# A four-layer conditional residual kernel: expert gates by way of DRAM, the place of the second group's routing, and the width of layer 3's second products

## The chip, the cores and the metric

The kernel runs on one core of a Trainium2 chip. The metric is device time in microseconds of one execution. Before the change the median of three runs is 597.46 us (597.17 to 600.03). The profiled execution took 598.18 us, of which the profile shows a span of 596.40 us on the core.

The core's engines work side by side and meet at semaphores: TensorE (PE; its weight loads are listed as PEld), VectorE (DVE), ScalarE (ACT), GpSimd (POOL), and SyncE (SP), which here only issues DMAs. Each engine does its own instructions in the order in which they were written.

## The reference

`x` has 8 sequences of 256 tokens and 1024 features. Four layers are added to it in turn. Cut to what matters:

```python
# L0: a shared matrix, plus 8 experts of rank 16, the best two of them by token
logits = einsum('btd,ed->bte', x, Wr) + 5.0 * one_hot(lang)[:, None, :]
topw, topi = top_k(logits, 2)
gates  = sum(one_hot(topi, 8) * softmax(topw)[..., None], axis=-2)
h      = einsum('btd,erd->bter', x, A)
x = x + einsum('btd,od->bto', x, W) + 2.0 * einsum('bter,bte,eor->bto', h, gates, B)
# L1: a weight plus a sign mask with a coefficient by sequence
x = x + einsum('bsi,oi->bso', x, W1) + b1 + einsum('bsi,bio->bso', x, 2 * mask - 1) * coeff
# L2: a full weight by sequence, chosen among 8 adapters
x = x + einsum('bsi,boi->bso', x, w2[ids])
# L3: rank 16 by sequence: down to 16 ranks, and up again
Bx = einsum('bni,bri->bnr', x, B3[ids])
x = x + einsum('bnr,bor->bno', Bx, A3[ids])
```

## The kernel before

**Tiling.** Features lie on partitions: `x` is 8 blocks (`K`) of 128 features. Two sequences make a pair of 512 tokens (`N`), two pairs make a group, and there are two groups. All large products are in float32r, each operand split in a high and a low part (`whi` and `wlo`, `hl`), and three of the four partial products are added up. ScalarE casts the high part (`highs`, L291), VectorE subtracts to get the low one (`lows`, L297), 4 and 3 items ahead of TensorE. The residual is folded into the weights: GpSimd adds the identity to a diagonal block (L241).

**Stages.** For each group: 16 slots of layer 0 (a product scheme with seven quarter products, `product` at L627), then for each pair 16 units of layer 1 and 16 of layer 2 (`main` at L907). A unit is one output block of 128 features for one sequence. The order is written out by hand: `l0_works` (L701) names what the other engines do at each slot, `l0_mids` (L790) what TensorE does in the middle of a slot's product, and `main` and `side` (L972) say the same by unit number `u` from 0 to 15. A work under a negative number comes ahead of that slot's casts. Pair numbers: `pair_of(g, 0)` is 1 and 3, `pair_of(g, 1)` is 0 and 2; in `l0_works` they are `p0` and `p1`.

**Gates of layer 0.** `logits` (L307) multiplies x with the router's weights in 32-column pieces of TensorE, into a PSUM bank. `router` (L318) on VectorE transposes them and finds the best two, `weigh` (L352) makes the weights, with one exponential on ScalarE, and transposes the gates to rows. The gates must then stand on 128 partitions, one for each (expert, rank). For pair 1 TensorE does that (`gates_by_transpose`). For the pairs 0, 2 and 3, `expand` (L384) writes the 128x128 tile to DRAM, and `gates_by_rank` (L401) reads it back, one DMA for each expert, the row repeated for 16 ranks. All of these DMAs are in SyncE's queue, along with weight loads, mask loads and stores. `gate` (L416) multiplies them with the experts' hidden values, `split_gates` (L409) makes the high and low part, and the `lora` products in slots 5, 9, 13 and 15 use them. In group 1 the logits of both pairs come in the last layer-2 units of the group before (q=1, u=13), router and weights at u=14 and 15, `expand` at slot 0, the reads at slots 3 and 6.

**Layer 3.** `proj_pair` (L445) and `proj` (L496) are the projections down to rank 16, also in 32-column pieces, four partial sums on four groups of partitions. `rank_pair` (L461) adds those four with a selection matrix, once for each of three blocks of 32 partitions; then the second product (`finish`, L476) multiplies 96 rows, which hold the partial products of high and low parts, 256 tokens at a time. For the pairs 0, 1 and 2 this work is put into the runs of later units or slots as `fillers`; the last pair goes by sequence and ends the kernel. `load_l3` and `prep_l3` (L428, L435) load and split the adapters, one tile for each sequence. Outputs are stored by SyncE.

PSUM has four auxiliary banks (`bank`, numbers 0 to 3) that logits, gates, experts and layer 3 share.

Of the kernel before, what the change touches and what calls it, by code (L numbers as in the profile page):

```python
# [12 lines left out]
ALU = mybir.AluOpType  # L13
# [21 lines left out]
def kernel(ctx: ExitStack, tc: tile.TileContext, x, lang, coeff, ids,  # L35
# [55 lines left out]


    sel = cst.tile([P, R], F32, name="sel")
    nc.vector.tensor_copy(sel, ident[:, :R])
    for g in range(1, 4):
        tt(sel, sel, ident[:, 32 * g:32 * g + R], ALU.add)
    sel3_raw = cst.tile([P, 96], F32, name="sel3_raw")
    nc.vector.memset(sel3_raw, 0.0)
    for c in range(3):
        nc.vector.tensor_copy(sel3_raw[:, 32 * c:32 * c + R], sel)  # L100
    sel3 = cst.tile([P, 96], FR, name="sel3")
    nc.vector.tensor_copy(sel3, sel3_raw)

# [203 lines left out]
    def logits(p):  # L307

        a, j = p // 2, 1 - p % 2
        pls[p] = bank(j, f"pl{p}")  # L310
        for k in range(K):
            for g in range(4):
                mm(pls[p][32 * g:32 * g + 32, :P], wrs[:, k, :],  # L313
                   X[a][:, j, k, g * P:(g + 1) * P], start=(k == 0), stop=(k == K - 1))
# [64 lines left out]

    gts, gates, phs, by_rank = {}, {}, {}, {}  # L380

    gts, gates, phs, by_expert = {}, {}, {}, {}

    def expand(p):  # L384

        by_expert[p] = dram.tile([P, P], F32, tag=f"gates{p}", name=f"gates{p}")
        nc.sync.dma_start(by_expert[p], gxs.pop(p))

# [12 lines left out]
    def gates_by_rank(p):  # L401

        gts[p] = gp.tile([P, N], F32, tag="lg", name=f"gt{p}", bufs=3)
        src = by_expert.pop(p).rearrange("(g e) t -> e g t", g=4)
        for e in range(E):
            nc.sync.dma_start(gts[p][e * R:(e + 1) * R].rearrange("r (g t) -> r g t", g=4),  # L406
                              src[e:e + 1].to_broadcast([R, 4, P]))

# [19 lines left out]
    def load_l3(b):  # L428
        raw = rawp.tile([96, K * P], F32, tag="w1", name=f"a3raw{b}", bufs=2)
        nc.sync.dma_start(raw, a3[bass.ds(adapter(b), 1)].rearrange("a r o -> (a r) o"))  # L430
        bt = l3p.tile([P, K, 32], F32, tag="b3", name=f"b3_{b}")
        nc.sync.dma_start(bt, b3[bass.ds(adapter(b), 1)].rearrange("a p k r -> (a p) k r"))
        l3raw[b], l3b[b] = raw, bt

    def prep_l3(b):  # L435
        raw = l3raw.pop(b)
        at = l3p.tile([96, K * P], FR, tag="a3", name=f"a3_{b}")
        copy(at, raw)
        tt(at[64:96, :], raw[64:96, :], f32(at[64:96, :]), ALU.subtract)
        l3[b] = at  # L440

# [19 lines left out]
    def rank_pair(q, n, banks):  # L461
        hi, lo = prs.pop(q)
        pr = bank(n, f"pr{q}")
        mm(pr[:96], sel3, hi, start=True, stop=False)
        mm(pr[:96], sel3, lo, start=False, stop=True)
        rt = l3p.tile([96, N], FR, tag="rt", name=f"rt{q}", bufs=1)
        copy(rt, pr[:96])
        tt(rt[32:64, :], pr[32:64, :], f32(rt[32:64, :]), ALU.subtract)
        for j in range(2):
            for m in range(0, K, 2):  # L470
                fillers.append(lambda b=2 * q + j, m=m, n=banks[m // 2 % len(banks)]: finish(
                    b, m, rt[:, (b % 2) * T:(b % 2 + 1) * T], n))

    stores = []

    def finish(b, m, rt, n):  # L476
        at = l3[b]
        xt = xts[b]
        po = bank(n, f"pf{b}_{m}")
        for i in range(2):  # L480
            mm(po[:, i * T:(i + 1) * T], at[:, (m + i) * P:(m + i + 1) * P], rt, start=True,  # L481
               stop=True)
        xs = xt[:, m:m + 2, :].rearrange("p m t -> p (m t)")
        tt(xs, po, xs, ALU.add)
        stores.append(lambda: nc.sync.dma_start(out[b, :, m:m + 2, :], xt[:, m:m + 2, :]))

# [9 lines left out]
    def proj(b, h, n):  # L496
# [9 lines left out]
        if h == 1:  # L506
# [3 lines left out]
            if last:  # L510

                raw = gp.tile([P, T], F32, tag="lg", name="pbraw", bufs=3)
                copy(raw, pb[:, :T])
                sums[b] = lambda: mm(pr[:96, :T], sel3_raw, raw, start=True, stop=False)
                return
# [5 lines left out]
            def both():  # L521
                mm(pr[:96, :T], sel3, hi, start=True, stop=False)
                mm(pr[:96, :T], sel3, lo, start=False, stop=True)
            sums[b] = both

    def third(b):

        pr = prs.pop(b)
        rt = l3p.tile([96, T], FR, tag="rt1", name=f"rt{b}", bufs=2)
        copy(rt, pr[:96, :T])  # L530
        tt(rt[32:64, :], pr[32:64, :T], f32(rt[32:64, :]), ALU.subtract)
        return rt


    b3_last = wrs[:, :3, :]

    def last_block():
        nc.vector.tensor_copy(b3_last, l3b[NB - 1][:, K - 1:, :].to_broadcast([P, 3, 32]))

    def rank(b):  # L540
        sums.pop(b)()
        rt = third(b)
        for m in range(0, K, 2):
            fillers.append(lambda m=m: finish(b, m, rt, (0, 2)[m // 2 % 2]))
# [156 lines left out]
    def l0_works(g):  # L701
# [46 lines left out]
        else:  # L748
            at(0, *both(s1_add), *both(less, "T1", 1, 0))
            at(3, *subs("S2", "A11", "S1"))  # L750
# [4 lines left out]
        else:  # L755
            at(0, lambda: expand(p0), lambda: expand(p1))
            at(3, lambda: gates_by_rank(p0))
# [32 lines left out]
    def l0_mids(g):  # L790
# [3 lines left out]
        if g == 0:  # L794
            return {3: lambda: logits(p1), -3: lambda: [gates_by_transpose(p0), router([p1]),
                                                        sub(0, "S2", "A11", "S1", 1)]}
        mids = {0: lambda: proj_pair(1, 0), 1: lambda: rank_pair(1, 1, (0, 1))}
        mids.update({s: lambda: fill(2) for s in (3, 4, 5, 7)})
        return mids
# [109 lines left out]
    def main(n):  # L909
# [16 lines left out]
        else:  # L926
# [6 lines left out]
            if q % 2:  # L933
# [4 lines left out]
                if u in (5, 7):  # L938
                    mid = [lambda: fill(4)]
            if q == 1:  # L940
                if u == 13:
                    mid = [lambda: [logits(p) for p in (2, 3)]]
            if q == 3:
# [28 lines left out]
    def side(n):  # L972
# [6 lines left out]
        if q % 2 == 0:  # L979
            if u < 2:  # L980
                load_l3(b + u)
            if u in (4, 5):
                prep_l3(b + u - 4)
            if u in (2, 5, 8, 11):
# [3 lines left out]
        if u in l:  # L988
            load_l3(b + u - l[0])
        if u in p:  # L990
            prep_l3(b + u - p[0])
        if q == 3 and u == p[1] + 1:
            last_block()
        if q == 1:
# [8 lines left out]
            if u in (14, 15):  # L1003
                la_parts(1, 4 * (u - 14), 4 * (u - 14) + 4)
            if u == 14:
                router([2, 3])
            if u == 15:
                weigh([2, 3])

# [88 lines left out]
    for n in range(len(slots)):  # L1098
# [5 lines left out]
    b = NB - 1  # L1104
    at, xt = l3[b], xts[b]
    sums.pop(b)()
    fill()
    store()
    mm(prs[b][:96, :T], b3_last.rearrange("p a b -> p (a b)"), xt[:, K - 1, :], start=False,
       stop=True)  # L1110
    ends = [ps.tile([P, 2, N], F32, tag="mm", name=f"ends{i}") for i in range(2)]
    by_act = (K - 2, K - 1)
    place = {m: ends[0][:, i, :T] for i, m in enumerate(by_act)}
    for m in by_act:
# [4 lines left out]
                  3: half(leave[1], 1), 4: half(leave[2], 0), 5: half(leave[2], 1)})  # L1119
    rt = third(b)  # L1120
    for m in (0, 1, *by_act, 2, 3, 4, 5):
# [73 lines left out]
```

## Time and profile before

| | before |
|---|---|
| median of three runs | 597.46 us |
| profiled execution | 598.18 us |
| its span on the core | 596.40 us |
| TensorE busy | 588.5 us, 99% |
| VectorE busy | 473.9 us, 79% |
| ScalarE busy | 382.7 us, 64% |
| GpSimd busy | 130.2 us, 22% |
| DMA | 131.22 MB, mean 220 GB/s |

Start times count from the start of the span. A row of a timeline gives start, length, engine, line, operation, output and inputs with their sizes, the number of instructions merged in it, and in brackets the idle time of the engine before it and what ended it. A row of the chain of work that ended last gives start, length, engine, output, line and number of records. Line L625 is the helper `link` that issues all large products, and L69 the helper of all element-wise operations of VectorE, so such rows are told apart by their tiles. A matmul in plain float32 appears as two records. Modelled ends of matmuls overlap their successors, so the distance of two starts is the price of one.

### The profile page before, as it was taken

How to read it: one execution, taken by the hardware profiler on the slowest of the kernel's cores; microseconds unless marked ns; L12 is line 12 of the kernel's file. 1: busy time of each engine (PE TensorE's matmuls, PEld its weight loads, DVE VectorE, ACT ScalarE, POOL GpSimd, SP SyncE). 2: the span in 40 equal slices, each digit the busy share in tenths (PEclk: the TensorE clock that was granted, in tenths of full speed). 3: DMA queues.
4: the chain of work that ended last, by engine and by line, in shares of the span. 5: the costliest groups of instructions: out<-in, count | busy, mean ns of one | idle time of the engine just before them, and what ended most of it. 6: DMA issues, size and time to landing. Idle time of an engine off the chain costs nothing.

```text
span 596.4 us, 9317 instructions
## 1 busy us (share of the span) xinstructions
PE 588.5 (99%) x3406; PEld 501.5 (84%) x3406; DVE 473.9 (79%) x563; ACT 382.7 (64%) x453; POOL 130.2 (22%) x178
## 2 busy tenths in 40 slices
PE   9999999999999999999999999999999999999995
PEld 7888788888888888888878888888888888888984
DVE  6687688899699999585855786789968999966863
ACT  5658466687669886543553865668866888864431
POOL 2313170113131014113110235411322110321000
PEclk9999999999999999999999999999999999999999
DMA  8978994566685877499950799835767676846704
GB/s 286 328 178 161 230 269 145 202 254 238 233 274 177 300 261 250 166 362 351 274 99 33 159 221 281 240 107 211 296 197 260 205 281 243 308 152 182 241 1 141
DMA packets 41886, 131.22 MB, mean 220 GB/s; under 512 B 5234, under 2 KB 8818, under 8 KB 41074
## 3 DMA queue, kind: packets, MB, share of 16 engines
q1 hardware_dynamic: 36946, 113.34, 54.6%
q0 software_dynamic: 4608, 16.78, 14.9%
q8 instruction: 26, 0.43, 0.3%
q10 hardware_dynamic: 288, 0.52, 0.3%
q14 instruction: 18, 0.15, 0.1%
HBM read 122.04 MB, written 8.59 MB: 219 GB/s over the span
## 4 chain that ended last, share of the span: by engine, by line
PE 93%; DMA 3%; DVE 1%; SPq 1%; ACT 1%; issue 0%; DVEq 0%; ACTq 0%
PE po L625 59%; PE mm L625 26%; PE pl L313 1%; PE pf L481 1%; DMA A<-in_w 1%; PE pb L453 1%; DMA gt<-gates 1%; PE ph L654 1%; PE ph L655 1%; PE ph L656 1%; SPq L406 1%; DVE wlo L69 1%; DMA gates<-gx 1%; PE pb L504 0%; PE po L572 0%
## 5 line engine op out<-in xcount | busy, mean ns | idle before, releaser
L625 PE MATMUL po<-hl,whi 128*128 128x512 f32 x1016 | 243.7, 391 | 0.0
L625 PEld LDWEIGHTS po<-hl,whi 128*128 128x128 f32 x1016 | 186.4, 188 | 35.8
L69 DVE TENSOR_TENSOR wlo<-raw,whi 128x1024 fp32r<-128x1024 f32 x128 | 160.6, 1263 | 2.8 <-issue 2.4
L294 ACT CAST whi<-raw 128x1024 fp32r<-128x1024 f32 x128 | 133.7, 1048 | 18.1 <-PE mm L625 8.3
L625 PEld LDWEIGHTS po<-hl,wlo 128*128 128x128 f32 x1016 | 130.5, 191 | 6.3 <-issue 1.4
L625 PE MATMUL po<-hl,wlo 128*128 128x256 f32 x1016 | 133.2, 283 | 0.0
L625 PE MATMUL mm<-whi,whi 128*128 128x512 f32 x224 | 87.9, 392 | 0.2 <-ACT whi L868 0.2
L263 ACT ACTIVATE raw<-raw,negc,c 128x1024 f32<-128x1024 int32 x64 | 79.6, 1243 | 13.0 <-DMA raw<-in_mask 12.8
L625 PE MATMUL mm<-wlo,whi 128*128 128x512 f32 x224 | 87.5, 390 | 0.0
L241 POOL TENSOR_TENSOR raw<-raw,ident 128x128 f32<-128x128 f32 x72 | 53.0, 738 | 129.6 <-DMA raw<-in_w 109.2
L625 PE MATMUL mm<-whi,wlo 128*128 128x512 f32 x224 | 70.6, 391 | 0.0
L69 DVE TENSOR_TENSOR raw<-raw,w 128x1024 f32<-128x1024 f32 x56 | 69.4, 1239 | 0.8 <-issue 0.8
L241 POOL TENSOR_TENSOR w<-w,ident 128x128 f32<-128x128 f32 x28 | 28.5, 1019 | 164.1 <-DMA w<-in_w 119.9
L69 DVE TENSOR_TENSOR wlo<-x,whi 128x1024 fp32r<-128x1024 f32 (+1 forms) x38 | 44.5, 1179 | 17.1 <-PE mm L625 9.8
L598 ACT COPY c<-po 128x512 f32<-128x512 f32 (+1 forms) x34 | 18.8, 552 | 50.8 <-PE po L625 50.8
L625 PEld LDWEIGHTS mm<-whi,whi 128*128 128x128 f32 x224 | 42.0, 188 | 10.5 <-issue 0.8
L625 PEld LDWEIGHTS mm<-whi,wlo 128*128 128x128 f32 x224 | 42.0, 188 | 9.4 <-DVE wlo L69 0.7
L625 PEld LDWEIGHTS mm<-wlo,whi 128*128 128x128 f32 x224 | 42.1, 188 | 8.8 <-DVE wlo L69 0.2
L294 ACT CAST whi<-A 128x1024 fp32r<-128x1024 f32 x26 | 27.3, 1049 | 26.1 <-PE mm L625 15.7
L294 ACT CAST whi<-x 128x1024 fp32r<-128x1024 f32 x34 | 35.3, 1048 | 10.8 <-PE mm L625 9.8
L601 ACT ACTIVATE sum<-po,b_sb 128x512 f32<-128x512 f32 (+1 forms) x36 | 23.1, 642 | 29.6 <-PE po L625 29.6
L69 DVE TENSOR_TENSOR wlo<-A,whi 128x1024 fp32r<-128x1024 f32 (+3 forms) x37 | 36.5, 1002 | 5.7 <-ACT whi L294 5.6
(128 smaller groups left out, 505.8 us busy)
## 6 DMA issues: line engine op xcount, KB each, us to landing
raw<-in_mask SPq DMA_DIRECT2D x64, 512.0 KB, 5.3
raw<-in_w SPq DMA_DIRECT2D x64, 512.0 KB, 4.5
w<-in_w SPq DMA_DIRECT2D x28, 512.0 KB, 3.3
out<-c SPq DMA_DIRECT2D x29, 256.0 KB, 7.1
A<-in_w SPq DMA_DIRECT2D x14, 512.0 KB, 9.2
x<-in_x SPq DMA_DIRECT2D x6, 1024.0 KB, 8.0
A<-in_w POOLq DMA_DIRECT2D x12, 512.0 KB, 9.4
x<-in_x POOLq DMA_DIRECT2D x12, 512.0 KB, 8.4
```

Of the source, the lines that this page charges most:

```text
L69: nc.vector.tensor_tensor(o, a, b, op)
L241: (eng or nc.gpsimd).tensor_tensor(t, t, ident, ALU.add)
L263: nc.scalar.activation(f32(raws[n]), raws[n], AF.Identity, bias=negc[:, b:b + 1], scale=c2[:, b:b + 1])
L294: copy(prep_hi(i), flat(source(i)))
L313: mm(pls[p][32 * g:32 * g + 32, :P], wrs[:, k, :], X[a][:, j, k, g * P:(g + 1) * P], start=(k == 0), stop=(k == K - 1))
L406: nc.sync.dma_start(gts[p][e * R:(e + 1) * R].rearrange("r (g t) -> r g t", g=4), src[e:e + 1].to_broadcast([R, 4, P]))
L453: mm(pb[c:c + 32, j * T:(j + 1) * T], l3b[b][:, k, :], xts[b][:, k, :], start=(k < 4), stop=(k >= 4))
L481: mm(po[:, i * T:(i + 1) * T], at[:, (m + i) * P:(m + i + 1) * P], rt, start=True, stop=True)
L598: copy(xs, po[:, :, T:])
L601: nc.scalar.activation(xs, po[:, :, T:], AF.Identity, bias=b1c)
L625: mm(*args, skip_group_check=True, **kw)
L654: mm(phs[p], hi, v[0][:, kk], start=(k == 0), stop=False)
```

## The change

Four things change.

1. `expand` writes the gates of a pair to a DRAM tile of 8 experts by 512 tokens, with four DMAs (one for each 128 tokens) in place of one of 128x128; `gates_by_rank` reads all of it with one DMA, each expert's row repeated for 16 partitions, in place of eight.
2. In group 1 the logits leave the layer-2 unit u=13 of pair 1 and stand in the middle of slot 0, directly before `proj_pair(1, 0)`; both pairs' logits share bank 1. The router moves from u=14 to slot 1, the weights from u=15 to slot 2, `expand` from slot 0 to slot 2. The negation of `T1` with its accumulating loads moves from slot 0 to slot 1, since it overwrites x.
3. For the pairs 0, 1 and 2, layer 3's second products take both sequences at once: 512 tokens with 128 rows, the upper 64 rows for one sequence and the lower 64 for the other. The selection matrix has zeros (`sel_of`), so each sequence's half of `rt` has zero rows under the other's adapter. The low parts are made over all 128 rows by one `scalar_tensor_tensor` with a column of 0 and -1 (`low_a`, `low_r`); a pair has one adapter tile, prepared once. All four partial products of the parts are now added up.
4. The last pair uses the same 128-row form, one sequence at a time, and the adapter array in DRAM has 64 rows for each adapter instead of 96.

```diff
-    sel3_raw = cst.tile([P, 96], F32, name="sel3_raw")
-    nc.vector.memset(sel3_raw, 0.0)
-    for c in range(3):
-        nc.vector.tensor_copy(sel3_raw[:, 32 * c:32 * c + R], sel)
-    sel3 = cst.tile([P, 96], FR, name="sel3")
-    nc.vector.tensor_copy(sel3, sel3_raw)
+    sel4 = cst.tile([P, 192], FR, name="sel4")
+    nc.vector.memset(f32(sel4), 0.0)
+    nc.vector.tensor_copy(sel4[:, 64:128].rearrange("p (c r) -> p c r", r=R),
+                          sel.rearrange("p (o r) -> p o r", o=1).to_broadcast([P, 4, R]))
+    sel_of = [sel4[:, 64:192], sel4[:, 0:128]]
+    low_a = cst.tile([P, 1], F32, name="low_a")
+    low_r = cst.tile([P, 1], F32, name="low_r")
+    for t, w in ((low_a, R), (low_r, 2 * R)):
+        nc.vector.tensor_reduce(
+            t, ident.rearrange("p (a b c) -> p a b c", b=2, c=w)[:, :, 1, :], AX.XY, ALU.add)
+        nc.vector.tensor_scalar(t, t, -1.0, None, ALU.mult)
...
     def logits(p):
         a, j = p // 2, 1 - p % 2
-        pls[p] = bank(j, f"pl{p}")
+        if p == pair_of(1, 0):
+            pls[p] = pls[p - 1][:, P:2 * P]
+        else:
+            pls[p] = bank(j, f"pl{p}")
...
     def expand(p):
-        by_expert[p] = dram.tile([P, P], F32, tag=f"gates{p}", name=f"gates{p}")
-        nc.sync.dma_start(by_expert[p], gxs.pop(p))
+        by_expert[p] = dram.tile([E, N], F32, tag=f"gates{p}", name=f"gates{p}")
+        gx = gxs.pop(p)
+        for g in range(4):
+            nc.sync.dma_start(by_expert[p][:, g * P:(g + 1) * P], gx[32 * g:32 * g + E])
...
     def gates_by_rank(p):
         gts[p] = gp.tile([P, N], F32, tag="lg", name=f"gt{p}", bufs=3)
-        src = by_expert.pop(p).rearrange("(g e) t -> e g t", g=4)
-        for e in range(E):
-            nc.sync.dma_start(gts[p][e * R:(e + 1) * R].rearrange("r (g t) -> r g t", g=4),
-                              src[e:e + 1].to_broadcast([R, 4, P]))
+        src = by_expert.pop(p).rearrange("e (o t) -> e o t", o=1).to_broadcast([E, R, N])
+        nc.sync.dma_start(gts[p], src)
...
-    def prep_l3(b):
-        raw = l3raw.pop(b)
-        at = l3p.tile([96, K * P], FR, tag="a3", name=f"a3_{b}")
+    def low_rows(t, low, whole):
+        nc.vector.scalar_tensor_tensor(t, f32(t), low, whole, ALU.mult, ALU.add)
+
+    def prep_l3(q):
+        raw = l3raw.pop(q)
+        at = l3p.tile([P, K * P], FR, tag="a3", name=f"a3_{q}", bufs=1)
         copy(at, raw)
-        tt(at[64:96, :], raw[64:96, :], f32(at[64:96, :]), ALU.subtract)
-        l3[b] = at
+        low_rows(at, low_a, raw)
+        l3[q] = at
...
     def rank_pair(q, n, banks):
         hi, lo = prs.pop(q)
         pr = bank(n, f"pr{q}")
-        mm(pr[:96], sel3, hi, start=True, stop=False)
-        mm(pr[:96], sel3, lo, start=False, stop=True)
-        rt = l3p.tile([96, N], FR, tag="rt", name=f"rt{q}", bufs=1)
-        copy(rt, pr[:96])
-        tt(rt[32:64, :], pr[32:64, :], f32(rt[32:64, :]), ALU.subtract)
         for j in range(2):
-            for m in range(0, K, 2):
-                fillers.append(lambda b=2 * q + j, m=m, n=banks[m // 2 % len(banks)]: finish(
-                    b, m, rt[:, (b % 2) * T:(b % 2 + 1) * T], n))
+            ts = slice(j * T, (j + 1) * T)
+            mm(pr[:, ts], sel_of[j], hi[:, ts], start=True, stop=False)
+            mm(pr[:, ts], sel_of[j], lo[:, ts], start=False, stop=True)
+        rt = l3p.tile([P, N], FR, tag="rt", name=f"rt{q}", bufs=1)
+        copy(rt, pr)
+        low_rows(rt, low_r, pr)
+        for m in range(0, K, 2):
+            n2 = [banks[(m + i) % len(banks)] for i in range(2)]
+            fillers.append(lambda m=m, n2=n2: finish_pair(q, m, rt, n2))
...
+    def finish_pair(q, m, rt, n):
+        xt2 = xts[q, 2]
+        for i in range(2):
+            po = bank(n[i], f"pf{q}_{m + i}")
+            mm(po, l3[q][:, (m + i) * P:(m + i + 1) * P], rt, start=True, stop=True)
+            xs = xt2[:, :, m + i, :]
+            tt(xs, po.rearrange("p (b t) -> p b t", b=2), xs, ALU.add)
+        for j in range(2):
+            stores.append(lambda b=2 * q + j, xt=xt2[:, j]: nc.sync.dma_start(
+                out[b, :, m:m + 2, :], xt[:, m:m + 2, :]))
...
-            at(0, *both(s1_add), *both(less, "T1", 1, 0))
+            at(0, *both(s1_add))
+            at(1, *both(less, "T1", 1, 0))
...
-            at(0, lambda: expand(p0), lambda: expand(p1))
+            at(1, lambda: router([p1, p0]))
+            at(2, lambda: weigh([p1, p0]), lambda: expand(p0), lambda: expand(p1))
...
-        mids = {0: lambda: proj_pair(1, 0), 1: lambda: rank_pair(1, 1, (0, 1))}
-        mids.update({s: lambda: fill(2) for s in (3, 4, 5, 7)})
+        mids = {0: lambda: [logits(p1), logits(p0), proj_pair(1, 0)],
+                1: lambda: rank_pair(1, 1, (0, 1))}
+        mids.update({s: lambda: fill(1) for s in (3, 4, 5, 7)})
...
-            if q == 1:
-                if u == 13:
-                    mid = [lambda: [logits(p) for p in (2, 3)]]
...
-            if u in (4, 5):
-                prep_l3(b + u - 4)
+            if u == 5:
+                prep_l3(q)
...
-            if u == 14:
-                router([2, 3])
-            if u == 15:
-                weigh([2, 3])
```

## The prediction

> **What bounds the kernel.** I read the page first, then the chain of work that ended last in order of time, then the timelines of the single engines around the three places that the change touches. Of the page:
>
> ```profile
> span 596.4 us, 9317 instructions
> PE 588.5 (99%) x3406; PEld 501.5 (84%) x3406; DVE 473.9 (79%) x563; ACT 382.7 (64%) x453; POOL 130.2 (22%) x178
> PE 93%; DMA 3%; DVE 1%; SPq 1%; ACT 1%; issue 0%; DVEq 0%; ACTq 0%
> ```
>
> TensorE sets the time; its clock row is at 9 in all 40 slices (granted clock 0.999). So an edit counts by the TensorE time that it takes out or adds, and by the waits of TensorE that it opens or closes. A modelled matmul lasts 391 ns but its successor starts earlier, so I take prices from runs in the chain (start us, length us, records):
>
> ```profile
> 247.98 1.86 PE pb L453 x32
> ...
> 285.83 3.63 PE pl L313 x128
> ...
> 298.52 2.72 PE mm L625 x12
> 301.24 2.45 PE pb L453 x32
> 303.69 2.93 PE mm L625 x12
> ...
> 324.79 0.48 PE pf L481 x4
> ```
>
> A 512-wide product costs 2.72/12 = 0.2267 us. A 256-wide one of layer 3 costs 0.48/4 = 0.120. The same projections (`proj_pair`) cost 1.86 us in L2 but 2.45 in group 1's slot 0: 0.59 us there is waiting. TensorE's weight loads name VectorE's `c` before L453 (0.5 us, once): the last output of pair 1 is late.
>
> The third place is group 0's gates of pair 0 (`gates_by_rank(p1)`), shown by the SyncE queue, the chain, VectorE and TensorE:
>
> ```profile
> 47.76 0.33 SPq L387 DMA_DIRECT2D gates<-gx  x1
> 51.08 5.37 SPq L406 DMA_DIRECT2D gt<-gates  x8
> 55.90 5.89 DMA gt<-gates
> 62.07 0.69 DVE L69 TENSOR_TENSOR gt<-ph,gt 128x512 f32<-128x512 f32 x1 [3.07 <-DMA raw<-in_mask]
> 62.56 0.61 PE L625 MATMUL mm<-whi,wlo 128*128 128x512 f32 x2
> 63.47 2.14 PE L625 MATMUL mm<-ghi,lb 128*128 128x512 f32 x8 [0.29 <-ACT ghi L412]
> 65.69 1.21 PE L625 MATMUL mm<-glo,lb 128*128 128x512 f32 x4
> ```
>
> Eight reads leave one after another until 56.45, the last lands at 61.8, and only then can VectorE multiply (the chain names the gates; the masks, which the wait names, were queued behind them). Two matmuls from 62.56 end at 63.01; the next starts at 63.47: 0.46 lost. Eight from 63.47 need 1.81, until 65.28; the low part starts at 65.69: 0.41 lost. Together 0.87 us.
>
> **The parts, against the profiled execution's 598.18 us (span 596.40 and 1.78 around it).**
>
> *Second products 512 wide.* Pairs 0, 1 and 2 have 16 products of 256 each, and get 8 of 512: 24 times, two of 0.120 become one of 0.2267, 0.0133 each, together -0.32. [...] The zero rows change only the partitions used (96 to 128), not the columns that stream; the 128-row rows of the same widths have the same pitch, so 0. The sums in `rank_pair` go from two of 0.235 to four of about 0.12, three times: 3 x 0.01 = +0.03. `prep_l3` drops four copies (1.05 us) on ScalarE and four subtractions (1.27) on VectorE; `scalar_tensor_tensor` for `tensor_tensor` costs nothing (227 against 226 ns on 128x64). None of it is on the path while TensorE is busy. Setting up `low_a`, `low_r`, `sel4`: two reductions over 64 values at 0.22, two small scalars at 0.16 and a longer memset, some 0.5 us more than before; VectorE's setup ended at 2.97 and its first `wlo` waited until 4.42, which covers it. Without that cover it would cost 0.5. In the last chain, behind the last `pr`, the parts of `rt` are 128 rows instead of 32 or 96, 256 columns: 0 (0.42 us for 128x256 and for 32x256).
>
> *Logits join the projections.* 128 records (3.63 us) leave the L2 unit u=13 and come before `proj_pair(1, 0)`. The work itself is 0. One change to and from the 32-column form is saved: around `pl`, the starts of the neighbouring runs lie 0.08 and 0.10 us further apart than in an undisturbed pair: -0.18. The wait of 0.59 goes: `c` gets 3.6 us more from the logits, and VectorE, which spent 5.3 us on router and weights just ahead of it, has that free. -0.59; both ends are 0 and -0.59.
>
> *What the move makes late.* Times here count from the start of group 1's slot 0. Slot 0 lasts 9.49 + 3.63 - 0.59 = 12.53; slots 1 to 4 end at 19.8, 26.6, 33.9 and 37.1 (their lengths as before). VectorE in slot 1: two `wlo` until 14.6, router 3.6 until 18.2. Its transposes come first and free bank 1 at about 15.2; TensorE needs that bank for `rank_pair` at 16.6, so 1.4 spare. Queued behind the router on VectorE: `rt` (needed only at 30.7, in slot 3) and the next `wlo` (start 19.6, when buffers come free). Slot 2: the second `wlo` waits for ScalarE until 22.0 as before and ends at 23.3; `weigh`, 1.67, until 24.9. Now SyncE: `expand` issues 4 + 4 writes, about 0.4 each (the two before took 0.80), so pair 3's until 26.6, pair 2's until 28.2. Nothing else waits in its queue there: stores start with slot 4, loads with slot 7. The writes land 1.6 (median) to 3.3 us after issue, 28.2 to 29.9; the one read is issued by 30.3.
>
> [...] The need:
>
> ```profile
> 327.66 2.36 DVE L69 TENSOR_TENSOR wlo<-x,whi 128x1024 fp32r<-128x1024 f32 x2 [1.30 <-issue]
> 329.94 0.69 DVE L69 TENSOR_TENSOR gt<-ph,gt 128x512 f32<-128x512 f32 x1
> 330.54 1.28 DVE L69 TENSOR_TENSOR c<-pf,c 128x512 f32<-128x512 f32 x2
> 332.44 0.64 PE L481 MATMUL pf<-rt,a 96*128 96x256 f32 x4
> ```
>
> The gate multiplies at 36.0 in the new count. Behind it on VectorE are the two additions that free banks 0 and 1, and TensorE needs those banks for the fill in slot 5, 0.6 us after they end. So the gates may land until 36.6 at no cost; each us beyond costs TensorE one us. I take 0, ends 0 and +2.3 (a read of 8.6 us, the longest in the trace, from 30.3). `T1`'s negation and its accumulating loads move by a slot, to 16.3 on ScalarE, landing (8.4 us) by about 25; slot 4's `whi` wants them at 34: 0.
>
> *Group 0's gates.* The four writes leave from 47.8 to 49.2, land by 52.5 (3.3 as before); the read leaves at 52.9. [...] Both waits go: -0.87; ends 0 and -0.87. SyncE is also free for the masks 3.2 us sooner, which nothing on TensorE waits for.
>
> Sum: -0.32 + 0.03 - 0.18 - 0.59 - 0.87 = -1.93. The profiled execution would be 596.25, and the median of runs 597.46 - 1.93 = **595.5** (the profiled one lies 0.72 above the median).
>
> **Rivals.**
> 1. *The gates of group 1 come late.* [...] Against: DMA is nearly empty there. With write and read both at the trace's longest 8.6 us, the write lands at 35.2, the read at 44.2, 7.6 too late: -1.9 + 7.6, 603.1. It turns the sign when the gates land 1.9 us after 36.6, and makes the kernel 0.5% slower from 41.5.
> [...]
> 3. *The waits only move*, to the next product: only the TensorE work counts, -0.47, 597.0.
> 4. *More slack pays elsewhere.* The long runs hold further small gaps: from 65.69, 196 records take 45.03 instead of 44.43; from 345.95, 240 take 54.86 instead of 54.41; two runs of 784 take 0.7 over their pitch each, 2.5 us together. If lighter VectorE, ScalarE and queues close half of them, 594.3. Against: no wait of TensorE is named there.
>
> **Chances.** Likeliest 0.45 (own range 595.2 to 596.4: upward the column rule, 0.26, and the wait of 0.59 kept; downward the 0.3 between the two lower runs of before); rival 1 0.15, rival 2 0.12, rival 3 0.08, rival 4 0.20. Half a per cent, 3.0 us, is about what a measurement of this kernel can tell. Faster by more is rival 4, 0.20; slower by more is rival 1, 0.15; the rest, 0.65, is within. The range leaves out most of rival 1 and reaches past rival 4's value and past no change: 593.9 to 598.3.
>
> **What would show it.** Right: `pb` in slot 0 at 1.86 us behind 128 records of `pl`; `mm<-ghi,lb` in group 0 without a wait; `pf` 0.227 us a record; the L1 and L2 runs unchanged. Wrong: a wait on `pf` or `ghi` in group 1's slot 5, `pr` waiting for a transpose in slot 1, or `gates<-gx` landing later than 3.3 us after the fourth issue.

## The result, and the profile after

The changed kernel takes 596.77 us (median of 22 runs, 595.54 to 598.11). The kernel before was run again beside it, 22 runs in all: 599.51 us (596.33 to 605.71). The ratio, which compares all runs and not the medians, is 0.995, 95% interval 0.9929 to 0.9972, so 1.7 to 4.3 us less. The prediction, made against the first three runs of before (597.46), had -1.9 us. How large the gain is depends on the runs of before that it is held against: beside the experiments below the kernel before ran 90 times more, and the median of all 112 runs is 598.83, which is 2.1 us above the changed kernel, not 2.7. Runs more than 1.5% above the fastest of their kernel are counted in medians and tables but left out of the ratios. Two things have to be explained: the gain in the profile, and why the runs of before spread over 9 us while those of the changed kernel keep within 2.6.

The profiled execution took 595.92 us against 598.18, its span 594.1 against 596.4. The page of the changed kernel:

```profile
span 594.1 us, 9230 instructions
PE 586.4 (99%) x3388; PEld 501.1 (84%) x3388; DVE 468.9 (79%) x561; ACT 379.0 (64%) x449; POOL 128.7 (22%) x178
PE 98%; DMA 1%; DVE 0%; ACT 0%; DVEq 0%; issue 0%; SPq 0%
```

The chain of work that ended last is TensorE's at 98%, where before 5% went by way of DMA, VectorE and SyncE: the detour through the gates in group 0 is gone. The rows of the chain that answer to those shown of before:

```profile
43.63 65.89 PE mm L661 x288
109.52 137.26 PE po L661 x784
246.79 1.86 PE pb L471 x32
260.45 0.91 PE pf L500 x4
293.40 2.72 PE mm L661 x12
296.12 3.63 PE pl L324 x128
299.75 1.73 PE pb L471 x32
301.48 2.94 PE mm L661 x12
322.60 0.45 PE pf L500 x2
```

From 43.63 one unbroken run leads to the first L1 unit. The projections behind the logits take 1.73 us, less even than the 1.86 of the same work in L2, where 128-column products stand ahead of it. A 512-wide second product takes 0.227. Group 0's gates, on SyncE's queue, VectorE and TensorE:

```profile
47.49 1.30 SPq L398 DMA_DIRECT2D gates<-gx  x4
51.03 0.71 SPq L416 DMA_DIRECT2D gt<-gates  x1
59.70 0.69 DVE L69 TENSOR_TENSOR gt<-ph,gt 128x512 f32<-128x512 f32 x1 [0.97 <-DMA gt<-gates]
62.28 0.62 PE L661 MATMUL mm<-whi,wlo 128*128 128x512 f32 x2
62.75 2.03 PE L661 MATMUL mm<-ghi,lb 128*128 128x512 f32 x8
64.62 1.09 PE L661 MATMUL mm<-glo,lb 128*128 128x512 f32 x4
```

Two matmuls from 62.28 end at 62.73; the high part starts at 62.75, the low part follows 1.87 later, where eight products at the pitch of 0.2267 need 1.81. No wait is left. In group 1 the moved work runs like this (VectorE, SyncE, VectorE, TensorE):

```profile
306.28 0.51 DVE L334 STREAM_TRANSPOSE lt<-pl 128x128 f32<-128x128 f32 x2
316.06 0.51 DVE L389 STREAM_TRANSPOSE gx<-lt 128x128 f32<-128x128 f32 x2
316.59 3.38 SPq L398 DMA_DIRECT2D gates<-gx  x8
320.15 0.67 SPq L416 DMA_DIRECT2D gt<-gates  x1
327.69 0.68 DVE L69 TENSOR_TENSOR gt<-ph,gt 128x512 f32<-128x512 f32 x1
330.14 0.61 PE L500 MATMUL pf<-rt,a 128*128 128x512 f32 x2
```

The gate's multiplication waits for no DMA (no bracket), and the fill of slot 5 comes in its turn.

Stage by stage, from the two chains:

| stretch | before | after | difference | forecast |
|---|---|---|---|---|
| start until `pg` in group 0 | 37.91 | 37.70 | -0.21 | 0 |
| `pg` until the first L1 unit of group 0 | 72.80 | 71.82 | -0.98 | -0.87 |
| three times `pf` and `pr` | | | -0.32 | -0.29 |
| logits leave u=13, slot 0's logits and projections | | | -0.91 | -0.77 |
| copy of the last `rt` until the first product behind it | 0.88 | 1.03 | +0.15 | 0 |
| sum | | | -2.27 | -1.93 |

Row four is made up of three pieces: slot 0 starts 3.82 us earlier against the fills before it (-5.12 + 1.30), the logits add 3.63 in their new place, and `pb` takes 0.72 less. The 0.21 at the start lies ahead of anything that the change touches except 0.5 us of setup on VectorE. It is no gain: over the 14 profiles of this study `pg` starts anywhere between 37.13 and 37.93.

### The profile page after: what moved, and what is told of

Read it like the earlier page. It is cut to its first block, busy times and chain, and to the rows that moved or that the text cites. A ratio compares the mean times of both kernels' runs of the same rounds, so it can differ in the third digit from the quotient of the medians.

```text
span 594.1 us, 9230 instructions
## 1 busy us (share of the span) xinstructions
PE 586.4 (99%) x3388; PEld 501.1 (84%) x3388; DVE 468.9 (79%) x561; ACT 379.0 (64%) x449; POOL 128.7 (22%) x178
## 4 chain that ended last, share of the span: by engine, by line
PE 98%; DMA 1%; DVE 0%; ACT 0%; DVEq 0%; issue 0%; SPq 0%
PE po L661 60%; PE mm L661 30%; PE pl L324 1%; PE ph L692 1%; PE ph L691 1%; PE ph L690 1%; PE pb L471 1%; PE pf L500 1%; DMA A<-in_w 1%; PE pb L538 0%; PE po L608 0%; DVE c L69 0%; PE pf L517 0%; PE po L613 0%; PE pr L485 0%; PE pr L484 0%
## 5 line engine op out<-in xcount | busy, mean ns | idle before, releaser
L249 POOL TENSOR_TENSOR raw<-raw,ident 128x128 f32<-128x128 f32 x72 | 54.7, 762 | 127.7 <-DMA raw<-in_w 88.5
L249 POOL TENSOR_TENSOR w<-w,ident 128x128 f32<-128x128 f32 x28 | 27.0, 964 | 165.5 <-DMA w<-in_w 97.1
L69 DVE TENSOR_TENSOR c<-mm,c 128x1024 f32<-128x1024 f32 x20 | 24.5, 1223 | 20.2 <-PE mm L661 20.2
```

The costliest lines, as they stand in the source:

```text
L69: nc.vector.tensor_tensor(o, a, b, op)
L249: (eng or nc.gpsimd).tensor_tensor(t, t, ident, ALU.add)
```

## Experiments

There are two theories for the gain. *Additive*: four separate pieces of TensorE's time go, as in the table. *Landing*: beyond that, the gates of the kernel before land at another time in every run, and TensorE pays for the late ones. The rival for the scatter (the spread of the runs) is the routing of group 1.

**The parts alone, and the kernel before once more.** The first experiment has only the new `expand` and `gates_by_rank`:

```diff
-        by_expert[p] = dram.tile([P, P], F32, tag=f"gates{p}", name=f"gates{p}")
-        nc.sync.dma_start(by_expert[p], gxs.pop(p))
+        by_expert[p] = dram.tile([E, N], F32, tag=f"gates{p}", name=f"gates{p}")
+        gx = gxs.pop(p)
+        for g in range(4):
+            nc.sync.dma_start(by_expert[p][:, g * P:(g + 1) * P], gx[32 * g:32 * g + E])
...
-        for e in range(E):
-            nc.sync.dma_start(gts[p][e * R:(e + 1) * R].rearrange("r (g t) -> r g t", g=4),
-                              src[e:e + 1].to_broadcast([R, 4, P]))
+        nc.sync.dma_start(gts[p], src)
```

> The kernel before with only the gates written by expert and read in one DMA. Additive theory: in the profile both waits ahead of the gates' products in group 0 go (0.46 and 0.41 us), nothing else on TensorE changes, so the stretch from the first logits to the start of group 0's first L1 unit is 0.9 to 1.0 shorter than in the profile of before and the span about 0.9 shorter. Landing theory for the scatter (runs of before lie between 596.3 and 605.7, runs of the changed kernel between 595.5 and 598.1): the eight reads land at times that vary from run to run, and TensorE waits for the last; then this part alone narrows the runs to within 3 us. If the scatter has its source in the routing of the second group, the runs of this kernel scatter as widely as those of before, by 5 us or more.

The second has only the move:

```diff
-            at(0, lambda: expand(p0), lambda: expand(p1))
+            at(1, lambda: router([p1, p0]))
+            at(2, lambda: weigh([p1, p0]), lambda: expand(p0), lambda: expand(p1))
...
-        mids = {0: lambda: proj_pair(1, 0), 1: lambda: rank_pair(1, 1, (0, 1))}
+        mids = {0: lambda: [logits(p1), logits(p0), proj_pair(1, 0)],
+                1: lambda: rank_pair(1, 1, (0, 1))}
```

> The kernel before with only the move: the logits in slot 0 of group 1 ahead of the projections, router in slot 1, weights and the writes (two of 64 KB) in slot 2, eight reads in slot 3. Additive theory: 0.7 less in slot 0's projections and 0.2 less around the old place of the logits, together -0.9; group 0's two waits stay. Rival (gates of group 1 late): with eight reads at 0.5 us apiece and 6 us to land, pair 3's gates land 1 us after they are needed and TensorE waits about 1 us at the fill of slot 5 or at the gates' products, so the sum is near 0. Scatter: as wide as before by the landing theory, narrow (3 us) if it is the routing's.

The third has only layer 3's new form (cut to the line of the second product):

```diff
-            mm(po[:, i * T:(i + 1) * T], at[:, (m + i) * P:(m + i + 1) * P], rt, start=True,
-               stop=True)
+            mm(po, l3[q][:, (m + i) * P:(m + i + 1) * P], rt, start=True, stop=True)
```

> The kernel before with only layer 3's new form (second products 512 wide for pairs 0 to 2, zero rows, one adapter tile for a pair). Additive theory: 24 products of 0.227 in place of 48 of 0.120, -0.3 on TensorE, and +0.15 in the last chain, where the low part now takes a scalar_tensor_tensor: -0.2 in all. [...] Scatter as wide as before by either theory of the scatter.

The fourth is the kernel before, with no edit:

> The kernel before, unchanged, for a second profile. Landing theory: the last of group 0's eight reads lands at another time than 61.8 us, and the waits ahead of the gates' products differ from 0.87 us by as much as the landing does (later than 59.9), while all other lengths of the chain stay within 0.1 us.

| kernel | median (lowest to highest), runs | over 602 us | ratio to before, 95% interval |
|---|---|---|---|
| gates alone | 597.05 (596.49 to 598.62), 18 | 0 | 0.9962 (0.9942 to 0.9982) |
| move alone | 598.45 (595.59 to 605.94), 19 | 6 | 1.0000 (0.9973 to 1.0026) |
| layer 3 alone | 598.83 (596.23 to 605.71), 22 | 5 | 0.9999 (0.9975 to 1.0024) |
| all of it | 596.77 (595.54 to 598.11), 22 | 0 | 0.9950 (0.9929 to 0.9972) |

The kernel before ran 52 times beside the first three rows (median 598.87, 6 over 602) and 22 times beside the last. The gates alone remove the scatter; the other two leave it, so it is not the routing's. Under that scatter the times can't show 0.9 or 0.3 us: 597.05 for the gates alone is within 0.3 of the whole change, in runs that were not made side by side. The traces do show it. From the start of the first L1 unit to the first product behind the last `rt`, a stretch that leaves out group 0's gates, the chains have (us):

| kernel | length | against before | expected |
|---|---|---|---|
| before | 478.25 | | |
| gates alone | 478.25 | 0.00 | 0 |
| move alone, three profiles | 478.36, 477.33, 477.32 | +0.11, -0.92, -0.93 | -0.9 |
| layer 3 alone | 478.09 | -0.16 | -0.2 |
| all of it | 477.13 | -1.12 | -1.1 (sum) |

So the pieces add up. The one misfit is the move's first profile: 1.0 us is lost between 267 and 297 us, where its chain runs through a load of adapters (`a3raw`) that took 11.21 us to land; the two repeats lack that. Ahead of this stretch the gates alone also lost 0.6 us between `pg` and the first gates' product of group 0, with a chain that runs through the load of `in_lb` (14.34 us to land); so did the second profile of before (0.6) and the move's first one (0.4). Late DMAs in other places can thus add to the scatter.

In the move's chain the logits and projections are the changed kernel's, with eight old reads behind them and no wait in slot 5 in this profile, against the 1 us of lateness that the rival gave it:

```profile
297.18 3.63 PE pl L316 x128
300.81 1.73 PE pb L456 x32
```

What moves most between executions is group 0. The second profile of the kernel before (VectorE, TensorE), whose execution took 601.08 us, and layer 3 alone:

```profile
63.94 0.69 DVE L69 TENSOR_TENSOR gt<-ph,gt 128x512 f32<-128x512 f32 x1 [4.71 <-DMA gt<-gates]
65.34 2.14 PE L625 MATMUL mm<-ghi,lb 128*128 128x512 f32 x8 [1.93 <-ACT ghi L412]
```

```profile
62.98 0.69 DVE L69 TENSOR_TENSOR gt<-ph,gt 128x512 f32<-128x512 f32 x1 [4.80 <-DMA raw<-in_mask]
64.38 2.13 PE L658 MATMUL mm<-ghi,lb 128*128 128x512 f32 x8 [2.02 <-ACT ghi L418]
```

(VectorE's wait of layer 3 alone names the masks, which are queued behind the gates.) Here TensorE waits 2 us, not 0.5, ahead of the high part. Layer 3 alone has the changed kernel's fills (0.91 and 0.45) and its longer last chain (1.03), so its -0.2 is in the trace and is swamped by this wait: its span was 596.9. The same execution of before also had a wait of 0.5 us at the gates of pair 2 in group 1, where the first profile had none; its stretch from the first L1 unit on is 1.14 us longer.

**How a late gate is paid.** Counted from the first gates' product of slot 5, all 14 profiles of the study, those of the experiments further down included, fall on one line (us; the packets are those of the gates' reads):

| kernel | packets | gate multiplied after | first L1 unit after |
|---|---|---|---|
| gates alone | 2 KB | 15.25 | 65.97 |
| changed | 2 KB | 16.23 | 65.89 |
| changed, last low part as before | 2 KB | 17.44 | 65.86 |
| changed, eight reads | 2 KB | 17.57 | 66.02 |
| changed, gates of group 1 late | 2 KB | 18.01 | 66.46 |
| move alone, three profiles | 512 B | 17.44, 17.49, 18.12 | 65.93, 65.93, 66.60 |
| changed, four reads, two profiles | 512 B | 17.56, 18.04 | 66.01, 66.52 |
| before, first profile | 512 B | 18.37 | 66.85 |
| layer 3 alone | 512 B | 19.93 | 68.40 |
| before, second profile | 512 B | 20.03 | 68.47 |
| before, five spare copies | 512 B | 23.05 | 72.54 |

Up to about 17.4 a landing costs nothing; from there on TensorE pays one us for one: 65.9 + (20.03 - 17.43) = 68.5. The last row lies 1.0 above the line, and has a reason of its own, below. So the forecast's -0.87 for this step was the value of one execution; over executions it lies between 0 and over 2. The large packets vary too, from 15.25 to 18.01, and once cost 0.5 us; what they lack in these profiles is the landing near 20.

> The move alone once more, for its profile: 6 of its 19 runs took 602.4 to 605.9 us, with a gap below them. If this profile falls there, the stall theory expects a wait of TensorE above 2.5 us ahead of a gates' product, and behind it a stretch at half the granted clock, as the experiment with the gates a slot later showed (a wait of 3.1 us, then 0.50), which jumps the time by some 2 us more; in every other profile the waits stay at 2.0 us or below and the clock at 1.0. If the slow group has another source, the loss is spread, or there is a lower clock with no wait ahead of it.

> The move alone a third time, for its profile; the theories expect the same as for its second. Where the gates of group 0 come at another time than 60.8 us, the wait ahead of their products moves with them, one us for one beyond about 60.9.

These two repeats of the move alone took 596.76 and 596.31 us. Neither fell above 602, so they show nothing about those runs; they gave two points of this table, whose line held in both, and the move's -0.92 and -0.93 above.

**Fewer issues, or fewer packets.** There are two edits of the changed kernel. By the issue theory the eight issues make the reads of before late, by the packet theory their 512 small packets: the first edit keeps the eight issues and has large packets, the second keeps the small packets and has four issues. The first makes eight reads by expert from the new layout, 128 packets of 2 KB in all:

```diff
-        src = by_expert.pop(p).rearrange("e (o t) -> e o t", o=1).to_broadcast([E, R, N])
-        nc.sync.dma_start(gts[p], src)
+        src = by_expert.pop(p).rearrange("e (o t) -> e o t", o=1)
+        for e in range(E):
+            nc.sync.dma_start(gts[p][e * R:(e + 1) * R].rearrange("r (o t) -> r o t", o=1),
+                              src[e:e + 1].to_broadcast([R, 1, N]))
```

> The changed kernel, its gates still written by expert, but read as before by eight DMAs, one for each expert: 16 rows of 2 KB each (128 packets in all, as in the one read; before there were 512 packets of 512 B). Issue theory: what made the reads late is that eight issues take 5 us of SyncE, so that the last leaves at about 55.5 instead of 51.7, when GpSimd's accumulating loads and the masks fill the DMA engines from 54 on; then this kernel waits in group 0 as before (0.5 to 3 us ahead of the gates' products, gates multiplied at 61 to 64 us) and its runs scatter by 5 us or more. [...]

The second makes four reads over all partitions from the old layout, 512 packets of 512 B in all. It also writes the gates as before, in one DMA (cut to the reads):

```diff
-        src = by_expert.pop(p).rearrange("e (o t) -> e o t", o=1).to_broadcast([E, R, N])
-        nc.sync.dma_start(gts[p], src)
+        src = by_expert.pop(p)
+        for g in range(4):
+            nc.sync.dma_start(gts[p][:, g * P:(g + 1) * P],
+                              src[32 * g:32 * g + E].rearrange("e (o t) -> e o t", o=1)
+                              .to_broadcast([E, R, P]))
```

> [...] Issue theory: four issues of about 0.6 us end at about 53, before the engines fill up; in time or nearly so, at most 0.5 us of waits, narrow runs (3 us). Packet theory: the 512 small packets land late, gates multiplied at 61 us or later, waits of 0.5 to 3 us and runs that scatter by 5 us or more.

The eight large-packet reads (SyncE, VectorE), then the four small-packet ones:

```profile
50.56 5.08 SPq L417 DMA_DIRECT2D gt<-gates  x8
60.57 0.69 DVE L69 TENSOR_TENSOR gt<-ph,gt 128x512 f32<-128x512 f32 x1 [2.34 <-DMA raw<-in_mask]
```

```profile
50.49 3.04 SPq L415 DMA_DIRECT2D gt<-gates  x4
61.60 0.69 DVE L69 TENSOR_TENSOR gt<-ph,gt 128x512 f32<-128x512 f32 x1 [2.88 <-DMA gt<-gates]
```

Eight reads in 5.08 us of issue: 596.58 us (595.62 to 597.73, 12 runs), ratio 0.9956 (0.9933 to 0.9979), none over 602. Four reads that are all issued 2 us sooner: 596.69 us, but 595.55 to 603.91, three of 12 at 603 to 604, ratio 0.9982 (0.9945 to 1.0019). The 29 runs of before beside both lie between 596.97 and 604.41. The read with the longer issue is the steady one, so the issue theory falls. The scatter goes with the small packets: over all runs on record, kernels with 512-byte packets had 29 of 168 over 602 us (before 15 of 112, move 6 of 21, layer 3 5 of 22, four reads 3 of 13), kernels with 2 KB packets 0 of 53 (changed, gates alone, eight reads, last low part as before; the two kernels whose edit itself delays the gates are left out). The layout of the writes changes together with the packets, so it is not ruled out; but in the two profiles here the first read leaves at 50.56 and 50.49, so the writes were done at the same time. The views of the queues from 46 to 66 us count 894 packets under 2 KB before and 182 in the changed kernel, 301 with the eight reads and 794 with the four. In the single profiles the difference of the reads is small (17.57 against 18.04 in the table, less than the packet theory had said):

> The four reads of 512-byte packets once more, for a second profile: 3 of its 12 runs took 603 us. Stall theory: if the profile is one of these, a wait above 2.5 us ahead of a gates' product and half the granted clock behind it; if not, gates multiplied in group 0 at 60 to 63 us and waits of 0 to 2 us.

```profile
60.55 0.69 DVE L69 TENSOR_TENSOR gt<-ph,gt 128x512 f32<-128x512 f32 x1 [2.41 <-DMA gt<-gates]
```

It took 595.79 us, and TensorE had no wait for these gates: one of the good executions. Why small packets sometimes land so late is not shown; the DMA engines are full there (DMA share 0.98 to 1.06 from 54 to 62 us in six profiles), with GpSimd's accumulating loads and the masks.

**The rival that was to end slower: group 1's gates late.** The changed kernel with weights, writes and first read one slot later:

```diff
-            at(2, lambda: weigh([p1, p0]), lambda: expand(p0), lambda: expand(p1))
+            at(3, lambda: weigh([p1, p0]), lambda: expand(p0), lambda: expand(p1))
             at(3, lambda: gates_by_rank(p0))
```

> The changed kernel with the second group's weights, writes and first read a slot later (weights in slot 3 behind two subtractions on VectorE). Rival 1's mechanism: pair 3's gates may land until 36.6 us after the start of slot 0 at no cost, and each us beyond costs one. Here VectorE has the gates at about 32.4, SyncE issues the read at about 36, and it lands 3.5 to 8 us later, at 39.5 to 44: TensorE waits 3 to 7.5 us at the fill of slot 5 (banks 0 and 1, behind the gate's multiplication on VectorE), and the span is longer than the changed kernel's by as much. If the gates have slack beyond what the prediction gave (TensorE goes on with other work), less than 2 us.

601.59 us (601.10 to 603.31, 10 runs), span 599.3 against 594.1. Two rows of the chain, then VectorE and TensorE:

```profile
327.97 4.09 DMA gt<-gates
334.02 0.50 PE pf L500
332.08 0.69 DVE L69 TENSOR_TENSOR gt<-ph,gt 128x512 f32<-128x512 f32 x1 [4.19 <-DMA gt<-gates]
333.42 1.10 PE L500 MATMUL pf<-rt,a 128*128 128x512 f32 x2 [3.06 <-DVE c L69]
```

The gates land at 40.0 after slot 0's start (292.07), 3.4 beyond the 36.6 that the prediction had as the limit, and TensorE waits 3.06 at the named place, for the additions that free the banks. The fill's second product waits for the second addition and starts at 334.02 only, so the fill is over at 334.52, 42.45 after slot 0's start. In the changed kernel it is over at 38.75 (slot 0 starts at 292.01):

```profile
330.31 0.45 PE pf L500 x2
```

The whole delay is thus 3.7 us for a landing that is 3.4 too late. The read lands 4.1 us after its issue. But the span is 5.2 longer, not 3.7. The stretches behind the wait (busy times of PE, PEld, DVE, ACT, POOL, then the granted clock of TensorE, DMA share and GB/s):

```profile
333.00:334.50 1.50, 0.99 (x3) 0.63 (x4) 1.50 (x4) 1.50 (x3) 0.00 (x0) 1.00 1.09 216
334.50:336.00 1.50, 1.50 (x7) 1.18 (x6) 1.50 (x3) 0.88 (x1) 0.00 (x0) 0.70 1.09 216
336.00:338.00 2.00, 2.00 (x7) 1.51 (x6) 2.00 (x4) 0.00 (x0) 0.88 (x1) 0.50 1.02 203
338.00:340.00 2.00, 2.00 (x9) 1.54 (x8) 1.16 (x2) 1.01 (x1) 0.00 (x0) 0.88 1.03 240
```

The clock fell to 0.50 some 1.6 us after work had begun again: the `ph` products of the chain stand 0.23 us apart until 335.21 and 0.42 from there on. The lost shares add up to 1.7 us ((1 - 0.70) x 1.5 + (1 - 0.50) x 2 + (1 - 0.88) x 2), which makes, by an estimate from these rows, 3.4 us at half the clock. From the fill of slot 5 to the next one TensorE takes 1.4 us more than in the changed kernel (13.90 against 12.46): that is the rest.

**A longer wait in group 0.** The kernel before, with five copies that nobody uses ahead of the eight reads:

```diff
         src = by_expert.pop(p).rearrange("(g e) t -> e g t", g=4)
+        if p == pair_of(0, 1):
+            for e in range(5):
+                spare = dram.tile([R, 4, P], F32, tag=f"spare{e}", name=f"spare{e}")
+                nc.sync.dma_start(spare, src[e:e + 1].to_broadcast([R, 4, P]))
```

> The kernel before with five spare copies of 32 KB, of the same packets, in SyncE's queue ahead of group 0's eight reads of gates (about 0.5 us of issue each, nobody uses them). Stall theory: the gates come about 2.5 us or more later than the 60.8 to 63.9 us seen so far, at 63.5 to 67, and TensorE waits 2.5 to 5 us ahead of their products; most runs then take 602 us or more, as in the slow group of the kernel before, and the profile shows half the granted clock behind the wait if that is above some 2.5 us. If the slow group has another source, the runs move by 1 to 3 us only, in step with the landing, and no half clock shows at such a wait.

605.16 us (603.83 to 607.22, 4 runs), ratio 1.0108 (1.0048 to 1.0168). VectorE, TensorE and the stretches:

```profile
66.52 0.69 DVE L69 TENSOR_TENSOR gt<-ph,gt 128x512 f32<-128x512 f32 x1 [7.93 <-DMA gt<-gates]
67.92 3.51 PE L629 MATMUL mm<-ghi,lb 128*128 128x512 f32 x8 [5.15 <-ACT ghi L416]
```

```profile
66.00:68.00 2.00, 0.09 (x1) 0.09 (x1) 1.48 (x2) 0.76 (x2) 0.00 (x0) 0.89 0.84 344
68.00:70.00 2.00, 2.00 (x5) 1.62 (x6) 2.00 (x4) 1.94 (x2) 0.00 (x0) 0.50 0.02 8
70.00:72.00 2.00, 2.00 (x8) 1.56 (x8) 2.00 (x3) 0.70 (x1) 0.00 (x0) 0.76 0.69 250
```

A wait of 5.15 us, then half the clock (0.50 from 68 to 70 us): eight products in 3.51 us instead of 2.14. The lost shares again add up to 1.7 us, by the same estimate 3.4 us at half the clock. At 603.83 us and above lie all four of its runs, and 9 of the 112 of the kernel before. So a late landing in group 0 is able to make such runs, by wait and clock together.

Whether the runs of before over 602 us are made by it was not seen: no profile fell among them. The clock on record for each run fits it. In the 24 runs over 602 of the kernels with small packets whose clock is listed, the mean granted clock of the whole run is 0.991 to 0.996 (mean 0.9934, mean time 604.1 us); in their 103 runs up to 600 us it is 0.995 to 0.999 (mean 0.9974, mean time 598.0). The ten runs with group 1's gates late have 0.991 to 0.996. By an estimate from these means the clock is worth 0.004 x 600 = 2.4 of the 6.1 us between the two sets, so a lower clock alone does not make such runs; a wait and a half clock behind it, as here, would make both parts. Where in the run it happens, the clock of a whole run can't say.

**The last chain.** The changed kernel with the last sequence's low part as before:

```diff
-        low_rows(rt, low_r, pr)
+        if b == NB - 1:
+            tt(rt[96:128, :], pr[96:128, :], f32(rt[96:128, :]), ALU.subtract)
+        else:
+            low_rows(rt, low_r, pr)
```

> The changed kernel with the last sequence's low part made by tensor_tensor on the 32 rows that are used, as before, in place of scalar_tensor_tensor on 128. If the scalar_tensor_tensor costs 0.06 us more with one input in PSUM, the step from the end of the last pr to the first product behind it is 0.06 to 0.15 shorter in the chain; if the longer step has another source (the weights' load, the 128 rows), it stays.

The chain of the changed kernel, then of this one:

```profile
586.03 0.49 DVE rt L449
586.52 0.14 issue
586.65 0.37 PE po L1153
```

```profile
586.20 0.44 DVE rt L69
586.64 0.04 issue
586.68 0.40 PE po L1156
```

From VectorE's start until the product: 0.62 against 0.48. So the +0.15 goes with the `scalar_tensor_tensor`: 0.05 longer, and 0.10 until TensorE goes on, which this swap takes away too. (The swap also goes from 128 rows to 32, and does not tell the two apart.) The span of 594.1 is unchanged, because this execution reached `pg` 0.16 later; from the first L1 unit on it is 477.02 against 477.13.

## Why the prediction was right, and where it was not

*What bounds the kernel, and the method.* Right. TensorE's time and waits were the right account; four copies, four subtractions and twelve DMAs fewer on the other engines appear nowhere in the chain.

*The number.* The measured 596.77 lies outside the 595.2 to 596.4 that the prediction gave to its likeliest case. Most of the miss of 1.3 us is its base: the three runs of before had a median of 597.46, the 112 runs have 598.83. Against these the gain is 2.1 us, near the forecast 1.93. Against the 22 runs the gain is 2.7; that this did not show in the miss is luck, as a base that was too low and a gain that was too small cancel in part.

*Second products 512 wide, -0.32; sums +0.03.* -0.32 measured for both: the fills fell from 0.96 to 0.91 and from 0.48 to 0.45, the sums from 0.47 to 0.47. The rows of the trace were the right source: in this kernel two 256-wide products (0.120 each) cost 0.0133 more than one of 512 (0.2267). The 0.26 by which the range reaches upward is shown by no run; 24 times the 0.0133 came out.

*Zero rows 0, and `scalar_tensor_tensor` 0.* The rows cost TensorE nothing (0.227 for a product). The instruction does: the term was sized by a row of 64 columns in SBUF. With one input in PSUM it takes 0.48 us for 128x256 against 0.42 for the old instruction on 32x256, and with what follows +0.15 in the last chain, the only place where it is not covered.

*Logits join the projections, -0.18 and -0.59.* -0.91 instead of -0.77. The wait went as forecast; the run of projections, which now stands directly behind other 32-column products, lost another 0.13 (1.86 to 1.73).

*What the move makes late, 0.* Right, nearly to the step: slots 1 to 4 end at 19.7, 26.5, 33.8 and 36.9 after slot 0's start (19.8, 26.6, 33.9, 37.1 forecast), the router's row at 14.3 (14.6), the weights' end at 24.6 (24.9), the last write's issue at 28.0 (28.2). The read left at 28.1 to 28.8, 1.5 sooner than the latest that was taken. When it would land was the author's estimate, with a term for the number of DMA engines behind a read that no run shows; in the runs the late read landed 4.1 us after its issue, and in the changed kernel VectorE did not wait for it. The limit of 36.6 and its price of one us for one held in the experiment (3.4 late, 3.7 of delay), but only for the wait itself: the clock made 5.2 us of it. Rival 1 would thus have crossed 0.5% sooner than the 4.9 us that the prediction gave: 3.4 us of lateness already cost 5.2.

*Group 0's gates, -0.87.* -0.98 in the profile. Both waits went; their size was that of one execution. The forecast treated the landing of 61.8 us as fixed; it varies, and so the step is worth from 0 to over 2 us, and more behind half a clock. Whether this makes the measured -2.7 out of -1.9 (-2.1 by the traces, without the start) is open: the interval of 1.7 to 4.3 holds all of these. The reason behind it, one issue in place of eight, was wrong for the scatter: eight issues with large packets are as steady. That both waits would go rests on a landing time estimated by the author with the same term for engines, which no run shows; in its place the runs show that the read was issued at 51.03, not 52.9, and that VectorE's wait for it ended at 59.7, 8.7 us later. Issued at 52.9, it would by an estimate from these numbers have landed at 61.6, hardly before the 61.8 of the kernel before: luck had a part.

How many DMA engines serve the one read is not shown. Between 46 and 66 us the view of the queues counts 269 packets under 512 B with the eight reads and 150 with the one, 119 fewer. Eight reads in place of one cost nothing that the times show (596.58 and 596.77 us).

*Rivals.* 1 did not happen; from 315 to 321 and from 321 to 327 us the DMA shares are 0.04 and 0.38 (0.00 and 0.06 before). 2 (596.4, no gain at group 0's gates) and 3 are refuted for the profiled executions: the waits went and did not come back. 4, more slack elsewhere, was given 0.20 and named a wrong place: the long runs of L1 and L2 are unchanged (137.26 us). What the change takes away beyond the forecast are the executions over 602 us, 15 of 112 before.

## What to carry to other kernels

A wait of half a microsecond for a DMA that shares full engines (DMA share 1.01 to 1.04 from 54 to 62 us before) was not half a microsecond here: it was one draw of a landing time. Look at the spread of the runs, and take a second profile, before that term goes into a sum. For a small transfer that is needed soon, try a layout in DRAM that makes its packets large, even if that costs several small writes; the number of issues mattered less here. And compare the lengths of single stretches between traces: where the times of the runs showed nothing, these agreed with the forecast to a few hundredths of a microsecond.

## What was not expected of the hardware

TensorE's granted clock fell to 0.50 behind waits of 3.06 and 5.15 us, and stayed at 1.00 behind waits of 0.5 and 1.93 us; behind 2.02 us eight products took 2.13 us, as behind 1.93 (2.14). The stretch behind the 1.93:

```profile
65.00:67.00 2.00, 1.66 (x7) 1.39 (x8) 2.00 (x3) 0.28 (x1) 0.00 (x0) 1.00 1.06 217
```

After the 3.06 us it fell not at once but about 1.6 us later, and cost 1.4 us more than the delay of 3.7. In both cases the lost shares of the clock come to 1.7 us, 3.4 us at half the clock by the estimate above. Why it falls behind 3.06 and 5.15 us and not behind 2.02, and why so late, is not shown. In these profiles a late landing thus has a step in its price between 2 and 3 us of wait.
